# Softmax denominators of an attention layer folded by an accumulating DMA, with smaller edits around it, in a two-layer fp32 kernel

## The chip, the cores and the metric

The kernel runs on one core of one Trainium2 chip, in fp32 throughout. The time is the device time of one execution of the whole program, in microseconds (us); the median of the runs counts. The engines are named as in the profile: PE (TensorE matmul), PEld (its weight loads), DVE (VectorE), ACT (ScalarE), POOL (GpSimd) and SP (SyncE, which issues most of the DMAs). One fp32 matmul instruction appears in the trace as two records, so that counts of records are twice the counts in the code.

## The reference

The input is 16 images of 256 channels and 32 x 32 pixels, that is 16 times a 256 x 1024 matrix. Two layers follow each other:

```python
# layer 0: attention, 4 heads of 64
qkv = (xs @ w_proj + b_proj).reshape(B, S, 4, 192)
q, k, v = split(qkv, 3, axis=-1)
attn = softmax(einsum('bihd,bjhd->bijh', q, k) * SCALE, axis=2)
x = (einsum('bijh,bjhd->bihd', attn, v) @ w_out + b_out + xs)
# layer 1: group norm, attention with 8 heads of 32, group norm, MLP of 1024
x = x + attention(group_norm(x, gn1_w, gn1_b), qkv_w, proj_w, proj_b, phys_bias)
h = gelu(mlp_w1 @ group_norm(x, gn2_w, gn2_b) + mlp_b1)
x = x + (mlp_w2 @ h + mlp_b2)
```

`phys_bias` is one number per head, added to the scores. The MLP is done with seven block products in place of eight (`make_blocks`, `mlp`).

## The kernel before, in words

`first_pass` does all images in one unrolled program. Channels lie on the 128 partitions in two halves (`CC` = 2), pixels in two blocks of 512 (`NT` = 2, `TB` = 512) or eight of 128 (`SB` = 8). Softmax is done without subtracting the maximum; `dsum` and `isum` collect the denominators and their inverses, and at the end one flag tells whether they stayed in range; `general_pass` would run only if they had not.

The order of the instructions is written out by hand. Each attention is a Python generator that yields once per step; `run` (L1036) draws from it, calls `later.tick()` at each step and puts pieces of other work (`fill`) behind the step. `Later.after(n, f)` (L37) runs `f` n ticks later. Each engine takes its instructions in the order so made; the queue of SP is one of them. A few instructions are placed by the tile framework's scheduler where they are likely to be ready, and `tc.issue_after` holds them behind a given instruction.

For each image b the stages are:

* `attention_a` (L384), layer 0, 32 steps: scores (L398), exp on ACT (L406), the sum of the exps over the key blocks on DVE (`es_a`, L431), the weighted values (L419). `cols[0]` = 32 makes other products use 32-column tiles meanwhile.
* The first MLP half of image b-1 (`hidden`: L906, gelu at L919), then query, key and first value products of layer 1 (`qkv_1`, L830).
* `attention_b` (L508), layer 1. An item (t, c) is a block of 512 queries and a half of the channels, that is four heads of 32. The items come in the order (1,0), (0,0), (0,1), (1,1). Each has four steps of two key blocks: scores of four heads on 32 x 64 tiles (L532), exps into `e` tiles (L547), sums over key blocks on DVE into two `es` tiles of 128 x 2 x 512 (`add`, L563), weighted values into `acc` (L584), added up in `res_b` (L595, L597). Behind each step `fill` puts the remaining products of layer 1's query, key and value (`own`), the second MLP half of image b-1 (`m`, L344, with 32-column tiles) and layer 0's query, key and value of image b+1. Only the first and the last image have little of this: the first has `own` alone, the last `own` and three MLP pieces.

After its last key block an item calls `normalise` (L601) one tick later: four matmuls of `eones` (128 x 32, the exponential of the bias) with the four 128 x 512 sums give the denominators `den_b`, each head's on 32 equal rows (L606). `denominators` (L357) then copies `den` to SBUF (L358, ACT), takes one row of each head to a 128 x 16 tile by DMA (L363, SP), one tick later inverts it (L367, DVE), writes it to DRAM (L368, SP), adds to `dsum` and `isum` (L369, L370, POOL) and broadcasts it back over 32 rows each (L373, four DMAs of 64 KB on SP). `scale` (L629) multiplies `res_b` with it and, after the second half of a block, sets off the projection `j` (`out_proj`, L660). The last item's steps fall into the next image's `attention_a`: its projection is handed over and done at step `SB + 4` there (L486).

Loads: `load_x` of the next image (1 MB) and `load_blocks(1, b-1)` (1.79 MB, L278) are written at the start of the loop over b (L1099 to L1103), before `attention_0` of that image; `load_blocks(2, b-1)` is written after the MLP's first half (L1119).

ACT has the functions Exp and Gelu in different tables. The compiler puts an `ACT_TABLE_LOAD` ahead of the first activation of each kind, so one ahead of the gelus and one ahead of the first exp of `attention_b` (listed under L547).

```python
den = bank(f"den_{key}_{i}", 1)
for g in range(G):
    nc.tensor.matmul(den[g * D : (g + 1) * D, :], k["eones"][:, c * G + g],
                     sums[i][g // 2][:, g % 2, :], start=True, stop=True)
```

Of the kernel before, what the change touches and what calls it, by code (L numbers as in the profile page):

```python
# [54 lines left out]
def kernel(  # L55
# [145 lines left out]
    ebias = const.tile([P, HEADS1], F32, name="ebias")  # L201
    eones = const.tile([P, HEADS1, D1], F32, name="eones")

    def exp_bias():
        nc.scalar.activation(ebias, pb, AF.Exp)
        nc.vector.tensor_copy(eones, ebias.unsqueeze(2).to_broadcast([P, HEADS1, D1]))


# [10 lines left out]
    with ExitStack() as first:  # L219
        first_pass(  # L220
            first, tc, x, out,
            dict(
                wp=wp, bqk=bqk, pb=pb, bo=bo, g1w=g1w, g1b=g1b, g2w=g2w,
                g2b=g2b, pjb=pjb, m1b=m1b, m2b=m2b, wo=wo, wq=wq, wpj=wpj,
                m2b2=m2b2, gavg=gavg, mhalf=mhalf, ones=ones, eones=eones,
                bvo=bvo, at_start=at_start, load_rest=load_rest, exp_bias=exp_bias,
                scale_v=scale_v,
                make_blocks=make_blocks,
                in_range=in_range,
            ),  # L230
        )
# [15 lines left out]
def first_pass(ctx, tc, x, out, k):  # L247
# [108 lines left out]

    def denominators(key, den, d, full, waits, then):  # L357
        nc.scalar.copy(d, den)  # L358
# [3 lines left out]
        row = dram.tile([4 * TB // n, n], F32, tag="row", name=f"row_{key}", bufs=4)  # L362
        nc.sync.dma_start(spread, d[::32].rearrange("p (a b) -> p a b", b=w))  # L363

        def invert():
            inverse = work.tile([P, w], F32, tag="inverse", name=f"inv_{key}", bufs=2)
            tc.keep_in_program_order(nc.vector.reciprocal(inverse, spread))  # L367
            nc.sync.dma_start(row.rearrange("r (a b) -> (r a) b", b=w), inverse)  # L368
            nc.gpsimd.tensor_add(dsum, dsum, spread)  # L369
            nc.gpsimd.tensor_add(isum, isum, inverse)  # L370
            num = P * n // (4 * TB)
            for r in range(P // num):
                nc.sync.dma_start(  # L373
                    full[r * num : (r + 1) * num], row[r].partition_broadcast(num)
                )
            later.after(waits[1], lambda: then(full))
# [7 lines left out]
    def attention_a(b, qT, kT, v, project):  # L384
# [3 lines left out]
        res = act.tile([P, CC, S], F32, tag="res", name=f"res_{key}")  # L388
        accs, held, sums = {}, {}, {}

# [18 lines left out]
        def weigh(i, kb, e):  # L409
# [19 lines left out]
            if kb == 1:  # L429
                sums[i] = work.tile([P, 2, TB], F32, tag="es", name=f"es_{key}_{i}", bufs=4)  # L430
            nc.vector.tensor_add(sums[i], held[i] if kb == 1 else sums[i], e)  # L431
# [76 lines left out]
    def attention_b(b, qT, kT, v, project):  # L508
# [3 lines left out]

        items = [(NT - 1, 0)]
        items += [(t, 0) for t in range(NT - 1)] + [(t, 1) for t in range(NT)]
        units = [(i, kb) for i in range(len(items)) for kb in range(0, SB, 2)]
        res, sums = {}, {}

# [35 lines left out]
        def add(i, kb, es, which):  # L553
            if kb == 0 and 0 in which:
                sums[i] = [
                    work.tile([P, 2, TB], F32, tag="es", name=f"es_{key}_{i}_{n}", bufs=4)
                    for n in range(G // 2)
                ]
            for n in which:
                if kb == 0 and n < G // 2:  # L560
                    continue
                d = sums[i][n % 2]
                ins = nc.vector.tensor_add(d, es[n % 2] if kb == 0 else d, es[n])  # L563
# [5 lines left out]
        def result(t):  # L569
            if t < NT - 1 and b == 0:  # L570
                return [
                    work.tile([P, TB], F32, tag="g", name=f"res_{key}_{t}_{c}", bufs=16)
                    for c in range(CC)
                ]
            tag = "res1" if t == NT - 1 else "res" if b < B - 1 else "q0"
            r = act.tile([P, CC, S if tag == "q0" else TB], F32, tag=tag, name=f"res_{key}_{t}")
            return [r[:, c, :TB] for c in range(CC)]

        def weigh(i, kb, es):
# [18 lines left out]
            if kb == SB - 2:  # L598
                later.after(1, lambda: normalise(i, r, i == len(items) - 1))

        def normalise(i, r, last):  # L601
# [3 lines left out]
            for g in range(G):  # L605
                nc.tensor.matmul(  # L606
                    den[g * D : (g + 1) * D, :],
                    k["eones"][:, c * G + g],
                    sums[i][g // 2][:, g % 2, :],
                    start=True,  # L610
                    stop=True,
                )
            full = work.tile([P, TB], F32, tag="full", name=f"rd_{key}_{i}", bufs=1)
            if at_end:
# [83 lines left out]
    def group_norm(key, src, stats, gw, gb, tag, out_tile, wait, then=None):  # L698
# [30 lines left out]
        def variances():  # L729
# [6 lines left out]
            nc.vector.tensor_mul(dv, dv, dv)  # L736
            tv = small.tile([P, CC], F32, tag="tv", name=f"tv_{key}")
            nc.vector.tensor_add(tv, dv, st["mv"][:, :, 1])
            st.update(mean=mean, tv=tv)
            later.after(1 if cols[0] == P else 5, apply)  # L740

        def apply():
# [3 lines left out]
            nc.gpsimd.tensor_tensor(rstd, rstd, k["mhalf"], ALU.pow)  # L746
            a = small.tile([P, CC], F32, tag="ga", name=f"ga_{key}")
            nc.vector.tensor_mul(a, rstd, gw)
            ma = small.tile([P, CC], F32, tag="gma", name=f"gma_{key}")
            nc.vector.tensor_mul(ma, st["mean"], a)  # L750
            c = small.tile([P, CC], F32, tag="gc", name=f"gc_{key}")
            nc.vector.tensor_sub(c, gb, ma)
# [16 lines left out]
    def qkv(key, D, src, weights, b_qk, qT, kT, v_dst):  # L769
# [17 lines left out]

        def v(n):
            ps = single(f"v_{key}_{n}")
            for i in range(2):  # L790
                sb = 2 * n + i
                for cc in range(CC):
# [6 lines left out]
                    )  # L799
            nc.scalar.copy(  # L800
                v_dst()[:, 2 * n : 2 * n + 2],
# [93 lines left out]
    def mlp(b, xb):  # L895
# [45 lines left out]

        def finish(i):
            ps = open_sums.pop(i)
            products_of(i, [(7, ps[:, 0, :], False), (6, ps[:, 1, :], False)])
# [5 lines left out]
            combine((1, 0), (0, 0), False, i)  # L950
            combine((0, 1), (1, 1), False, i)

        hidden = [
# [101 lines left out]

    nothing = work.tile([P, TB], F32, tag="full", name="nothing", bufs=1)
    nc.vector.memset(nothing, 0.0)
# [36 lines left out]
    later.after(2, fold_bias)  # L1094
    later.after(8, k["scale_v"])
    hidden, outputs = [], []
    last = NT * CC * SB // 2 - 1
    for b in range(B):
        if b + 1 < B:  # L1099
            xs[b + 1] = load_x(b + 1)  # L1100
        xn = []
        if b:
            load_blocks(1, b - 1)  # L1103
        run(
# [36 lines left out]
        if not first:  # L1141

            fill = {m: [piece] for m, piece in enumerate(own[:5:2] + own[1::2] + own[6:])}
            fill.update({len(own) + 3 * m: [piece] for m, piece in enumerate(now)})
            now = []
# [28 lines left out]
    for j, (what, most) in enumerate(((dsum, DEN_MAX), (isum, 1.0 / DEN_MIN))):  # L1174
        top = small.tile([P, 1], F32, tag="top", name=f"top_{j}")
        nc.vector.tensor_reduce(top, what, AX.X, ALU.add)
# [4 lines left out]
    nc.vector.tensor_scalar(ok[:32], count, P - 0.5, None, ALU.is_ge)  # L1181
    both = small.tile([P, 1], F32, name="both", bufs=1)
    nc.vector.tensor_mul(both[:32], ok[:32, 0:1], ok[:32, 1:2])
# [294 lines left out]
```

## Time and profile before

| | |
|---|---|
| median of 3 runs | 3666.58 us (3666.36 to 3667.38) |
| the profiled execution, its own time | 3666.7 us |
| its span in the trace | 3664.9 us |
| DVE, ACT, POOL busy | 2658.1, 2154.3, 129.5 us |
| granted PE clock | 0.999 |
| one image in the middle of the run (from one stage to the same stage of the next image) | 226.4 us |
| `den_b` matmuls (L606) | 512 records, 592 ns each |
| ACT_TABLE_LOAD of L547 | 15, of 1283 ns |

Busy is the time in which an engine has at least one instruction of its own running. Four matmuls on different column tiles run beside each other, so the mean time of one record is not what it costs; that is read from the distance between the starts of neighbouring groups. The chain of work goes back from the last instruction, at each step to what released it or to the instruction before it on its engine; a row of it is the start, the length in us, engine, tile, line. In the timeline a row also gives the shapes, the number of records, and in brackets the idle time of the engine before it and what ended that.

### The profile page before, as it was taken

How to read it: one execution, taken by the hardware profiler on the slowest of the kernel's cores; microseconds unless marked ns; L12 is line 12 of the kernel's file. 1: busy time of each engine (PE TensorE's matmuls, PEld its weight loads, DVE VectorE, ACT ScalarE, POOL GpSimd, SP SyncE). 2: the span in 40 equal slices, each digit the busy share in tenths (PEclk: the TensorE clock that was granted, in tenths of full speed). 3: DMA queues.
4: the chain of work that ended last, by engine and by line, in shares of the span. 5: the costliest groups of instructions: out<-in, count | busy, mean ns of one | idle time of the engine just before them, and what ended most of it. 6: DMA issues, size and time to landing. Idle time of an engine off the chain costs nothing.

```text
span 3664.9 us, 79373 instructions
## 1 busy us (share of the span) xinstructions
PE 3632.6 (99%) x34221; PEld 1346.2 (37%) x34221; DVE 2658.1 (73%) x3424; ACT 2154.3 (59%) x2832; POOL 129.5 (4%) x266
## 2 busy tenths in 40 slices
PE   9999999999999999999999999999999999999999
PEld 3433343333433334333343333434334343343433
DVE  4586777767777677776767777677777777767777
ACT  4665657556565655656556565564655656556572
POOL 3000000000000000000000000000000000000000
PEclk9999999999999999999999999999999999999999
DMA  4000110101101011010110101101011010100100
GB/s 147 10 17 29 55 33 14 51 30 54 33 14 51 30 54 33 14 51 31 53 33 20 51 27 51 33 19 50 27 51 33 19 50 29 50 33 31 47 28 27
DMA packets 66549, 138.36 MB, mean 38 GB/s; under 512 B 35630, under 2 KB 36398, under 8 KB 61966
## 3 DMA queue, kind: packets, MB, share of 16 engines
q1 hardware_dynamic: 63116, 126.64, 10.7%
q8 instruction: 270, 4.42, 0.5%
q0 software_dynamic: 1328, 6.17, 0.5%
q14 instruction: 89, 0.73, 0.1%
q10 hardware_dynamic: 1746, 0.40, 0.1%
HBM read 111.17 MB, written 21.23 MB: 36 GB/s over the span
## 4 chain that ended last, share of the span: by engine, by line
PE 91%; DVE 4%; ACT 3%; DMA 1%; issue 1%; SPq 0%; ACTq 0%; POOL 0%; DVEq 0%
PE s_a L398 12%; PE acc_b L584 12%; PE s_b L532 12%; PE acc_a L419 12%; PE m L344 10%; PE m L906 9%; PE qk_a L344 6%; PE qk_b L344 5%; PE v_a L344 3%; PE j L344 3%; PE v_b L344 2%; ACT e_b L547 2%; PE o L344 2%; PE den_b L606 1%; DVE g L962 1%
## 5 line engine op out<-in xcount | busy, mean ns | idle before, releaser
L563 DVE TENSOR_TENSOR es_b<-es_b,e_b 128x1024 f32<-128x1024 f32 x768 | 899.3, 1219 | 243.8 <-ACT e_b L547 243.8
L547 ACT ACTIVATE e_b<-s_b 128x1024 f32<-128x1024 f32 (+1 forms) x1280 | 982.9, 864 | 132.2 <-PE s_b L532 132.0
L406 ACT ACTIVATE e_a<-s_a 128x1024 f32<-128x1024 f32 x512 | 521.2, 1025 | 360.0 <-PE s_a L398 347.6
L398 PE MATMUL s_a<-q,k 64*64 64x512 f32 x4096 | 544.3, 593 | 0.0
L419 PE MATMUL acc_a<-e_a,v 64*64 64x512 f32 x4096 | 540.1, 589 | 0.0
L532 PE MATMUL s_b<-q,k 32*64 32x512 f32 x8192 | 519.7, 600 | 4.9 <-DVE res_b L597 1.6
L431 DVE TENSOR_TENSOR es_a<-es_a,e_a 128x1024 f32<-128x1024 f32 x384 | 473.9, 1234 | 64.8 <-ACT e_a L406 41.2
L584 PE MATMUL acc_b<-e_b,v 128*32 128x512 f32 x4096 | 492.1, 598 | 0.0
L344 PE MATMUL m<-g,w 128*32 128x512 f32 (+1 forms) x3320 | 404.3, 592 | 0.0
L532 PEld LDWEIGHTS s_b<-q,k 32*64 32x64 f32 x8192 | 170.9, 130 | 321.3 <-issue 130.9
L419 PEld LDWEIGHTS acc_a<-e_a,v 64*64 64x64 f32 x4096 | 187.9, 133 | 251.5 <-issue 218.4
L398 PEld LDWEIGHTS s_a<-q,k 64*64 64x64 f32 x4096 | 175.9, 133 | 246.7 <-issue 193.1
L563 DVE TENSOR_TENSOR es_b<-e_b,e_b 128x1024 f32<-128x1024 f32 x128 | 150.8, 1220 | 153.4 <-ACT e_b L547 153.4
L906 PE MATMUL m<-gn_h,w 128*128 128x512 f32 x512 | 243.7, 604 | 5.7 <-DVE g L932 3.3
L584 PEld LDWEIGHTS acc_b<-e_b,v 128*32 128x32 f32 x4096 | 108.5, 109 | 357.5 <-ACT e_b L547 194.7
L344 PE MATMUL qk_a<-x,wp 128*32 128x512 f32 (+1 forms) x1856 | 235.1, 593 | 4.1 <-ACT k L784 4.1
L344 PE MATMUL qk_b<-gn_g,wq 128*32 128x512 f32 (+1 forms) x1280 | 234.0, 592 | 0.0
L597 DVE TENSOR_TENSOR res_b<-res_b,acc_b 128x512 f32<-128x512 f32 x192 | 131.8, 686 | 129.8 <-PE acc_b L584 129.8
L344 PEld LDWEIGHTS m<-g,w 128*32 128x32 f32 (+1 forms) x3320 | 121.4, 112 | 262.3 <-issue 235.3
L962 DVE TENSOR_TENSOR g<-g,g 128x512 f32<-128x512 f32 x320 | 206.3, 681 | 4.0 <-ACT g L919 2.8
L906 PE MATMUL m<-hs,w 128*128 128x512 f32 x384 | 177.9, 592 | 0.1
L919 ACT ACTIVATE g<-g,m1b 128x512 f32<-128x512 f32 x128 | 92.2, 722 | 99.3 <-DVE g L946 72.2
(147 smaller groups left out, 2803.6 us busy)
## 6 DMA issues: line engine op xcount, KB each, us to landing
w<-w_kept SPq DMA_DIRECT2D x30, 1792.0 KB
d_a<-row_a SPq DMA_DIRECT2D x64, 256.0 KB
rd_b<-row_b SPq DMA_DIRECT2D x252, 64.0 KB
out_dram<-x SPq DMA_DIRECT2D x63, 256.0 KB
x<-in_x_dram SPq DMA_DIRECT2D x30, 512.0 KB
w_kept<-w_made POOLq DMA_DIRECT2D x2, 1792.0 KB, 6.0
w_made<-in_L_conv_mlp_w_dram POOLq DMA_DIRECT2D x8, 256.0 KB, 6.1
x<-in_x_dram SPq DMA_DIRECT2D x4, 256.0 KB
```

The costliest lines, as they stand in the source:

```text
L344: nc.tensor.matmul(o[sl], w[:, sl], r, **flags)
L398: nc.tensor.matmul(s[h : h + HALF, g, :], kT[g * D : (g + 1) * D, c, kb * P + h : kb * P + h + HALF], qT[g * D : (g + 1) * D, c, t * TB : ...
L406: nc.scalar.activation(e, s, AF.Exp, scale=float(D) ** -0.5)
L419: nc.tensor.matmul(accs[i][h][g * D : (g + 1) * D, :], v[h * HALF : (h + 1) * HALF, kb, c * 2 + g], e[h * HALF : (h + 1) * HALF, g, :], st ...
L431: nc.vector.tensor_add(sums[i], held[i] if kb == 1 else sums[i], e)
L532: nc.tensor.matmul(outs[g][h : h + HALF, :], kT[g * D : (g + 1) * D, c, k0 : k0 + HALF], qT[g * D : (g + 1) * D, c, t * TB : (t + 1) * TB] ...
L547: nc.scalar.activation(to, s, AF.Exp, scale=float(D) ** -0.5)
L563: ins = nc.vector.tensor_add(d, es[n % 2] if kb == 0 else d, es[n])
L584: nc.tensor.matmul(acc[g * D : (g + 1) * D, :], v[:, kb + m, c * G + g], es[2 * m + g // 2][:, g % 2, :], start=(m == 0), stop=(m == 1),)
L597: nc.vector.tensor_add(r, r, acc)
L906: nc.tensor.matmul(ps, blocks[1][number - 1][:, i * P : (i + 1) * P], inputs[b][number], start=first, stop=True, skip_group_check=not first,)
L962: (nc.vector.tensor_add if plus else nc.vector.tensor_sub)(d, d, gs[(*what, i)])
```

## The change

Three of an image's four items get their denominators in another way. `fold` copies the sums of the lower 64 partitions of `es` (64 x 4 x 512) over 128 partitions (128 x 2 x 512) with a DMA on SP, and a second DMA, issued by POOL, adds the upper 64 partitions to it. Three ticks after `fold`, `normalise_folded` multiplies the result with `folded`, whose columns say which head a partition holds: eight matmuls of 128 columns in place of four of 512. A head's denominators lie on 8 equal rows now, and the 512 queries as four groups of 128 rows by 128 columns; so `denominators` takes 16 rows to the 128 x 16 tile and writes the inverses with four DMAs (`parts`). The wait between the broadcast and `scale` is 2 ticks (4 for the third item). The last item of each image, and the third of the last image, are done as before. `packed` lies in the buffer with the tag "res", which the group norm's output `gn_g` holds before; that output is read by the products `qk_b` and `v_b`.

With it: the items go in the order (0,0), (0,1), (1,0), (1,1), and the results take other buffers; `full` has two buffers; the large loads are written 14 ticks into `attention_a`, behind the last broadcast; the copy of the first `v_b` goes to DVE; behind the last gelu of `hidden` a one-column Exp (`back_to_exp`) is put on ACT; in the first and last image `own` is spread in another way over the steps, and its last piece (`qk_b`) then stands at step 5. Some small tiles are shared.

```diff
+    def fold_ones():
+        nc.gpsimd.memset(folded, 0.0)
+        g_num = P // D1
+        w = D1 // g_num
+        for c in range(HEADS1 // g_num):
+            for g in range(g_num):
+                nc.gpsimd.dma_start(
+                    folded[g // 2 :: 2, c, g % 2, g * w : (g + 1) * w],
+                    eones[g // 2 :: 2, c * g_num + g, :w],
+                )
...
-    def denominators(key, den, d, full, waits, then):
+    def denominators(key, den, d, full, waits, then, parts=1):
...
-        nc.sync.dma_start(spread, d[::32].rearrange("p (a b) -> p a b", b=w))
+        nc.sync.dma_start(
+            spread, d[:: 32 // parts].rearrange("p (a b) -> p a b", b=w)
+        )
...
+            if parts > 1:
+                num = P // parts
+                for r in range(parts):
+                    nc.sync.dma_start(
+                        row[:, r * n // parts : (r + 1) * n // parts].rearrange(
+                            "g (a b) -> g a b", b=w
+                        ),
+                        inverse[r * num : (r + 1) * num],
+                    )
...
-                nc.sync.dma_start(
+                spread_out["last"] = nc.sync.dma_start(
...
-        items = [(NT - 1, 0)]
-        items += [(t, 0) for t in range(NT - 1)] + [(t, 1) for t in range(NT)]
+        items = [(t, c) for t in range(NT) for c in range(CC)]
...
             if kb == SB - 2:
-                later.after(1, lambda: normalise(i, r, i == len(items) - 1))
+                last = i == len(items) - 1
+                if last or b == B - 1 and t == NT - 1:
+                    later.after(1, lambda: normalise(i, r, last))
+                else:
+                    fold(i, r)
+
+        def fold(i, r):
+            if i == 0:
+                packs.append(act.tile([P, 4, TB], F32, tag="res", name=f"packed_{key}"))
+            packed = packs[0][:, i % 2 * 2 : i % 2 * 2 + 2]
+            nc.sync.dma_start(packed, sums[i][:HALF])
+            nc.gpsimd.dma_start(packed, sums[i][HALF:], accum_op=ALU.add)
+            later.after(3, lambda: normalise_folded(i, r, packed))
+
+        def normalise_folded(i, r, packed):
+            c = items[i][1]
+            q = TB // G
+            den = bank(f"den_{key}_{i}", 1)[:, :q]
+            for m in range(2):
+                for n in range(G):
+                    nc.tensor.matmul(
+                        den[n * D : (n + 1) * D, :], k["folded"][:, c, m],
+                        packed[:, m, n * q : (n + 1) * q], start=m == 0, stop=m == 1,
+                    )
+            full = work.tile([P, TB], F32, tag="full", name=f"rd_{key}_{i}", bufs=2)
+            denominators(
+                f"{key}_{i}", den, full[:, :q], full, (1, 2 if i < 2 else 4),
+                lambda full: scale(i, r, False, full), G,
+            )
...
+            copy = nc.vector.tensor_copy if not n and b_qk is None else nc.scalar.copy
...
+            if i == n4 - 1:
+                later.after(2, back_to_exp)
...
+        def back_to_exp():
+            one = small.tile([P, 1], F32, tag="part", name=f"one_{b}")
+            nc.scalar.activation(one, gs[1, 1, n4 - 1][:, :1], AF.Exp, scale=0.0)
...
+    later.after(9, k["fold_ones"])
...
-        if b + 1 < B:
-            xs[b + 1] = load_x(b + 1)
+        def load_next(b=b):
+            if not b:
+                xs[1] = load_x(1)
+                return
+            with tc.issue_after(spread_out["last"].ins):
+                load_blocks(1, b - 1)
+                if b + 1 < B:
+                    xs[b + 1] = load_x(b + 1)
+
+        later.after(14, load_next)
...
-            fill = {m: [piece] for m, piece in enumerate(own[:5:2] + own[1::2] + own[6:])}
+            fill = {0: own[:1], 1: own[1:3], 2: own[4:5], 3: own[5:6], 4: own[3:4], 5: own[6:]}
```

## The prediction

> **What bounds the kernel now.** I read the page first: busy times, then the chain that ended last.
>
> ```profile
> PE 3632.6 (99%) x34221; PEld 1346.2 (37%) x34221; DVE 2658.1 (73%) x3424; ACT 2154.3 (59%) x2832; POOL 129.5 (4%) x266
> ...
> PEclk9999999999999999999999999999999999999999
> ...
> PE 91%; DVE 4%; ACT 3%; DMA 1%; issue 1%; SPq 0%; ACTq 0%; POOL 0%; DVEq 0%
> ```
>
> PE has work nearly always, at full clock, and holds 91% of the chain. So a gain is either a matmul that is no longer done, or one of the few moments in which PE waits. The chain of one image from the middle, in order of time, shows what the denominators cost there:
>
> ```profile
> 1255.40 1.90 PE s_b L532 x32
> 1257.30 1.85 PE acc_b L584 x16
> 1259.15 0.86 PE den_b L606 x8
> 1260.01 3.43 PE m L344 x32
> 1263.45 1.90 PE s_b L532 x32
> ```
>
> Each step runs matmul to matmul without a gap, 7.19 us a step where nothing is added (1281.58 to 1288.77, from one `m` to the next `den_b`); an item adds 0.86 us. Third, the timeline where attention_b begins, the one place in an image where PE stands still:
>
> ```profile
> 1227.36 1.97 PE L532 MATMUL s_b<-q,k 32*64 32x512 f32 x32
> ...
> 1228.07 1.28 ACT L547 ACT_TABLE_LOAD   x1
> 1229.37 3.84 ACT L547 ACTIVATE e_b<-s_b 128x512 f32<-128x512 f32 x5
> 1230.02 1.93 PE L344 MATMUL v_b<-wq,gn_g 128*32 128x256 f32 x32 [0.68 <-ACT e_b L547]
> ...
> 1233.05 0.63 ACT L800 COPY v<-v_b 128x512 f32<-128x512 f32 x1
> ...
> 1233.73 1.98 PE L532 MATMUL s_b<-q,k 32*64 32x512 f32 x32
> ```
>
> The first exps wait for the table, `v_b` waits for an exp to free its bank (0.68 us), and the next scores wait for the copy of `v_b` behind the exps. The waits on PE's own row agree: `v_b` behind `e_b` is the longest, 10.2 us in 15 times.
>
> **The change part by part.** All against the profiled execution, 3666.7 us (1.8 us around its span; the median of the runs shown is 3666.58, the same).
>
> *Folded matmuls.* Removed per item: 4 matmuls of 512 columns, four column tiles beside each other, two records each: 0.86 us. Added: 8 of 128 columns, so each tile passes 4 records of 128 columns for 2 of 512, half the columns. That columns set the price shows in the chain: 32 records of 256 columns (`v_b`) take 1.73 us, 32 of 512 (`m`) take 3.43. So 0.43 us. Bounds: 0.43, and 0.86 from `den_a` (L450), which has as many instructions as the folded form and costs 0.86. I take 0.43, since `den_a` has 256 columns and fits the column rate itself. There are 3 folded items in 15 images and 2 in the last. In the 14 middle images all is on PE's path: 42 x 0.43 = 18.1 us. In the first and last image ACT paces most steps (PE waits for exps at 170.96 below), and I count nothing. ACT's copy of `den` shrinks from 619 ns; it isn't on the path.
>
> The Trainium skill, "TensorE: Matmul & The Clock Gate", section "Back-to-back issue gap", speaks against short matmuls: streams of load and matmul are said to come every 81 ns at 128 columns, where the isolated gap is 56. As an estimate from it, 4 records deep at that surplus of 25 ns make 0.1 us more, and 4 us less gain in all. The row of 256 columns shows no such surplus; no run here has 128.
>
> *The Exp put behind the last gelu.* The load (1.28 us) moves from 1228.07 to behind the last gelu, which ends at 1222.21. ACT is idle 1.13 us ahead of each of the next copies, so it fits beside PE's `qk_b` (7 us). Then the first exp starts when its scores are there: a step later exps start 1.13 us after `s_b` (1233.73, 1234.86), which makes 1228.49 for 1229.37. That is 0.88 us, and `v_b` and the next `s_b` follow the exps. 15 images: 13.2 us. Bounds: 0 if ACT's copies then hold PE, 1.28 if all of the load counts. The copy given to DVE falls into a DVE idle time of 9.38 us. In the last image the same Exp also stands in the tail on ACT; beside 24 us of unbroken PE products it costs nothing.
>
> The skill, "ScalarE: Activation LUTs", section "What ACT_TABLE_LOAD costs", puts a switch at 2.66 us, load and drain. The rows show 1.28 and an exp 0.02 us later. By the page this term would be up to 15 x 2.66, an estimate of 40 us; the measured row decides.
>
> *The two DMAs of a fold.* 512 KB by SP, then 512 KB added by POOL. In the middle images they lie under two steps. For the second item (old order) the last sum ends at 1285.75, `den_b` stood at 1288.77, and the folded one comes two ticks later, at 1303.2: 17.4 us of cover. The trace has no accumulating DMA. Nearest rows: 512 KB of `d_a<-row_a` 4.3 us; POOL's 256 KB loads 6.1 us, its 1 KB loads from 4.3; `sp_b` on SP 2.0 (1260.84 to 1262.83). Low end 2.0 + 4.3 = 6.3 us, high end 4.3 + 2 x 6.1 = 16.5 if reading two sources doubles POOL's time. I take 4.3 + 6.1 = 10.4, the rows nearest in size. All lie inside 17.4, so the middle images pay nothing.
>
> *The first and last image pay.* `packed` takes the buffer of `gn_g`, whose last reader is the `qk_b` now at step 5, and the folded `den_b` of item 0 is due at step 6: one `s_b` and one `acc_b` later. Rows of the first image:
>
> ```profile
> 165.37 1.90 PE L344 MATMUL qk_b<-gn_g,wq 128*32 128x512 f32 x16
> 167.20 1.97 PE L532 MATMUL s_b<-q,k 32*64 32x512 f32 x32
> 169.11 1.92 PE L584 MATMUL acc_b<-e_b,v 128*32 128x512 f32 x16
> 170.96 3.12 PE L532 MATMUL s_b<-q,k 32*64 32x512 f32 x32
> 174.01 1.92 PE L584 MATMUL acc_b<-e_b,v 128*32 128x512 f32 x16
> ```
>
> From the end of `qk_b` (167.1) to the `acc_b` of the step after: 6.9 us. With the pair of DMAs lasting D, `den_b` starts at D, 0.43 + about 1.9 for the scores, so that `acc_b` comes at D + 2.4: a loss of D - 4.5. Behind the waiting matmul stands all of PE's queue, and ACT, which paces these steps, runs dry. D = 10.4: 5.9 us in each of two images, 11.8. Bounds: 1.8 and 12 each. The three later folds of these two images have about 10.7 us (a sum ends at 175.46, `den_b` stood at 175.75, two steps of some 5 us more follow): 0 at 10.4, D - 10.7 each beyond, 5.8 at the high end.
>
> *At nothing.* SP: three more issues per fold for the inverses, 0.34 us each, in 7.19 us steps; `row` and the broadcasts land within the two ticks of 14 us. POOL: the accumulating DMA waits ahead of `dsum` and `isum`, for which nobody waits but the flag at the end; the group norm's power on POOL comes an attention later. Loads behind the last broadcast: 2.8 MB then have some 40 us until `hidden`, and go at 400 KB per us in the DMA times; what they no longer delay is DVE's `res_b` (waits for `rd_b`, 47.9 us in 14 times) in attention_a, where DVE has 1.23 us of sums per 1.72 us step, so PE gains nothing. If that cover were gone, PE would wait up to 4.7 us an image. `fold_ones` runs on POOL in the first image, far ahead of its use. The new spread of `own`: some 1 us either way.
>
> **Sum:** 18.1 + 13.2 - 11.8 = 19.5. 3666.7 - 19.5 = 3647.2, so 3647 us.
>
> **The rivals.**
>
> *The pair is quick* (D near 6.3 to 8): loss 1.8 to 3.5 in the two images, 31.3 - 3.6 = 27.7 at best: 3639 to 3643. For it: 8 KB trips of 2.0 us and loads at 400 KB per us. Against: POOL's 4.3 us at the least.
>
> *The pair is long* (12 to 14.5): 15 to 20 us lost on item 0 of the two images, 4 to 11 on their later folds: 31.3 - 19 = 12.3 to about 0, so 3654 to 3667.
>
> *The short matmuls save nothing* (0.86 stays, bound by instructions): 13.2 - 11.8 = 1.4, so 3665; no change. For it: `den_a`'s 16 records. Against: the 256-column rows.
>
> *Slower: PE waits for the accumulating DMA in every image.* In-order PE stands at `den_b` 42 times if D exceeds 17.4. The end images alone turn the sign at 14.5 (3677 at 16.5); beyond 17.4 each us costs 42 more. D = 20: 31.3 - 31 (item 0 twice) - 27.9 (three later folds) - 2.6 x 42 = -137, so 3804. For it: no row with addition, and a second source to read. Against: only doubling POOL's row reaches 16.5.
>
> *It doesn't do what it says*: the folded products stand in the code order two steps behind the item, so this is out but for the cases above.
>
> **How the numbers follow.** About 0.2% (7 us) is what a measurement can tell from no change. Forecast (D of 8 to 12, 3643 to 3654) 0.42; quick 0.29; long 0.11, half of it faster (0.05), the rest same (0.06); no saving 0.07, same; slower 0.11. Faster: 0.42 + 0.29 + 0.05 = 0.76. Same: 0.06 + 0.07 = 0.13. Slower: 0.11. The range leaves out the last two cases (0.18): 3637 to 3664; 2 us at the low end are for the spread of `own`.
>
> **What would show it.** Right: `den_b` of 0.43 us in the chain; the table load right behind the last gelu, and no wait of `v_b` for `e_b`; the image's period down from 226.4 to 224.3 us; two waits of PE of some 6 us on the accumulated tile, in the first and last image alone. Wrong: `den_b` groups of 0.6 us or more; waits of PE for that DMA in the middle images; no wait in the end images (the pair is quick); DVE late in attention_b, so that `j` waits.

## The result and the profile after

The changed kernel takes 3675.78 us (median of 13 runs, 3674.66 to 3679.81), the kernel before 3666.58 (13 runs, 3664.54 to 3667.77): a ratio of 1.0027, 95% interval 1.0019 to 1.0036. It is 9 us slower where 19.5 us less were forecast. The profiled execution took 3677.3 us, its span is 3675.3.

The first page hardly shows it. PE is as busy as before, and every slice of the clock row is a 9:

```profile
PE 3627.0 (99%) x34597; PEld 1357.1 (37%) x34597; DVE 2668.4 (73%) x3440; ACT 2131.0 (58%) x2833; POOL 217.4 (6%) x322
...
PEclk9999999999999999999999999999999999999999
...
PE 92%; DVE 5%; DMA 2%; ACT 0%; issue 0%; SPq 0%; ACTq 0%; POOL 0%; DVEq 0%
```

So I laid the two traces side by side by stage, from the first `s_b` or `s_a` of one to that of the next:

| stretch (us) | before | after | difference |
|---|---|---|---|
| the 14 middle images, in all | | | -29.0 |
| `attention_b` of the first image and the `attention_a` after it | 192.0 | 215.3 | +23.2 |
| last image, first `s_b` to last product | 168.3 | 180.2 | +11.8 |
| last product to the end of the span | 4.9 | 8.9 | +4.0 |
| start | | | +0.3 |

Before rounding they sum to 10.4, the difference of the spans. The middle images do what was forecast, 2.1 us an image; 1.4 of the 29.0 us is another matter, a wait of DVE for `d_a<-row_a` that stands in the third image of the kernel before and not here (more on it at e3). The chain of work there, in order of time:

```profile
1285.23 1.85 PE acc_b L604 x16
1287.09 0.44 PE den_b L639 x16
1287.53 3.43 PE m L357 x32
```

`den_b` is 0.44 for 0.86 us and nothing around it waits. All of PE's waits for `packed_b` (three, 16.0 us) fall in the end images. The whole loss lies at the two ends of the run. PE in the first image, at the first folded item:

```profile
163.68 1.98 PE L560 MATMUL s_b<-q,k 32*64 32x512 f32 x32
165.58 1.92 PE L604 MATMUL acc_b<-e_b,v 128*32 128x512 f32 x16
175.17 1.08 PE L639 MATMUL den_b<-packed_b,folded 128*32 128x128 f32 x16 [7.66 <-DMA packed_b<-es_b]
176.18 3.79 PE L560 MATMUL s_b<-q,k 32*64 32x512 f32 x32
```

This is the wait that was forecast, 7.66 us here and 7.43 in the last image:

```profile
3532.90 1.08 PE L639 MATMUL den_b<-packed_b,folded 128*32 128x128 f32 x16 [7.43 <-DMA packed_b<-es_b]
3533.91 4.14 PE L560 MATMUL s_b<-q,k 32*64 32x512 f32 x32
```

The row behind it says more: the same 32 records of `s_b` that took 1.98 us ahead of the wait take 3.79 here, 4.14 there. Asked for the stretches around it in steps of 3.41 us, the trace gives the reason (columns: stretch; its length, then busy time and records of PE, PEld, DVE, ACT, POOL; granted clock; DMA share; GB/s):

```profile
169.24:172.66 3.42, 0.00 (x0) 0.00 (x0) 2.43 (x3) 0.00 (x0) 0.52 (x1) 1.00 0.78 111
172.66:176.07 3.41, 0.90 (x16) 0.66 (x16) 0.00 (x0) 0.00 (x0) 0.00 (x0) 0.50 0.38 42
176.07:179.48 3.41, 3.41 (x36) 1.59 (x32) 0.15 (x1) 1.53 (x4) 0.21 (x1) 0.50 0.05 7
179.48:182.90 3.42, 3.42 (x34) 0.86 (x34) 2.09 (x3) 2.57 (x3) 0.00 (x0) 1.00 0.00 0
196.55:199.96 3.41, 1.66 (x22) 0.59 (x18) 1.76 (x3) 1.42 (x3) 0.00 (x0) 1.00 0.16 50
199.96:203.38 3.42, 2.70 (x30) 0.91 (x30) 3.42 (x5) 0.68 (x2) 0.22 (x1) 0.50 0.02 5
```

The granted clock is 0.50 for 6.8 us behind the wait, and again from 200.0 us on, behind a stretch in which PE was busy 1.66 of 3.41 us. There are four such stretches within the run: 6.8, 6.8 and 3.4 us in the first image, 10.2 in the last; 27.3 us in all at half clock. Before, there was none between start and tail. A slice of the page is 92 us long and rounds them away.

What made PE idle near 200 us is a second wait, on another engine. All engines of the first image:

```profile
186.01 0.56 SPq L629 DMA_DIRECT2D packed_b<-es_b  x1
...
186.62 3.92 SPq L388 DMA_DIRECT2D row_b<-inv_b  x4
...
191.79 4.17 SPq L400 DMA_DIRECT2D rd_b<-row_b  x4
...
198.20 0.69 DVE L679 TENSOR_TENSOR res_b<-res_b,rd_b 128x512 f32<-128x512 f32 x1 [4.07 <-DMA rd_b<-row_b]
...
200.68 3.71 PE L560 MATMUL s_b<-q,k 32*64 32x512 f32 x30 [1.52 <-DVE res_b L617]
```

The second item's 512 KB copy stands on SP's queue ahead of the first item's four small writes. These then take 3.92 us to issue, the broadcasts 4.17. For the third item, with no copy close ahead, it is 2.49 and 1.70:

```profile
240.84 2.49 SPq L388 DMA_DIRECT2D row_b<-inv_b  x4
...
244.50 1.70 SPq L400 DMA_DIRECT2D rd_b<-row_b  x4
```

The multiplication by the inverses, `scale`, stands on DVE two ticks behind the inversion, and in this image a tick is some 5 us: DVE has inverted at 185.90, stands at the multiplication 8.2 us later and waits 4.07 us, for the second item 5.36. Behind it in DVE's order is the `res_b` that frees `acc_b`'s bank, so PE waits too.

Third, the tail. All engines at the end:

```profile
3645.44 1.28 ACT L1005 ACT_TABLE_LOAD   x1
3646.74 0.20 ACT L1005 ACTIVATE one<-g 128x1 f32<-128x1 f32 x1
...
3649.36 0.16 DVE L1237 TENSOR_REDUCE top<-dsum 128x1 f32<-128x16 f32 x1
...
3666.34 0.22 PE L1241 MATMUL count<-ok,ones 128*32 128x2 f32 x2
```

The Exp of the last image writes a tile of the tag "part", and so does `top` now, the first step of the range flag. `top` comes behind the Exp, `count` behind the last product, and the program ends on the flag. Before, `count` was hidden among the products:

```profile
3609.38 0.22 PE L1180 MATMUL count<-ok,ones 128*32 128x2 f32 x2
```

### The profile page after: what moved, and what is told of

The parts are those of the page before. It is cut to its first block, busy times and chain, and to the rows that moved or that the text cites. A ratio compares the mean times of both kernels' runs of the same rounds, so it can differ in the third digit from the quotient of the medians.

```text
span 3675.3 us, 80535 instructions
## 1 busy us (share of the span) xinstructions
PE 3627.0 (99%) x34597; PEld 1357.1 (37%) x34597; DVE 2668.4 (73%) x3440; ACT 2131.0 (58%) x2833; POOL 217.4 (6%) x322
## 4 chain that ended last, share of the span: by engine, by line
PE 92%; DVE 5%; DMA 2%; ACT 0%; issue 0%; SPq 0%; ACTq 0%; POOL 0%; DVEq 0%
PE s_b L560 13%; PE acc_b L604 12%; PE s_a L425 12%; PE acc_a L446 12%; PE m L357 10%; PE m L954 7%; PE qk_b L357 6%; PE qk_a L357 6%; PE v_a L357 3%; PE v_b L357 3%; PE j L357 3%; PE o L357 2%; DVE g L1016 1%; PE den_a L479 1%; DMA d_a<-row_a 1%; DVE x L719 1%
## 5 line engine op out<-in xcount | busy, mean ns | idle before, releaser
L560 PE MATMUL s_b<-q,k 32*64 32x512 f32 x8192 | 528.8, 605 | 9.5 <-DVE x L719 2.9
```

What stands on the lines that cost most here:

```text
L560: nc.tensor.matmul(outs[g][h : h + HALF, :], kT[g * D : (g + 1) * D, c, k0 : k0 + HALF], qT[g * D : (g + 1) * D, c, t * TB : (t + 1) * TB] ...
```

## The experiments

My theory after reading the traces: all of the loss comes from the folds of the two end images (the wait, the half clock behind it, DVE's wait) and from the Exp in the tail. The rivals: the new order of the items and the new spread of `own` cost there; or the DMAs cost everywhere. Times are medians, beside 3675.8 (changed) and 3667 to 3668 (before, in the same sessions); the ratio is to the kernel before, with its 95% interval.

**Nothing folded in the end images** (e1).

```diff
-                if last or b == B - 1 and t == NT - 1:
+                if last or b in (0, B - 1):
                     later.after(1, lambda: normalise(i, r, last))
```

> The changed kernel, but in the first and the last image no item is folded: all four go the old way through es_b and eones. Theory (the whole loss lies in the folds of these two images: PE's wait for packed, the half clock behind it, DVE's wait for the broadcasts behind the second 512 KB DMA): attention_b of the first image back from 108.1 to about 90.5 us, attention_a of the second image from 107.1 to 101.8, the last image from 180.2 to about 168.5, the clock at 1.0 but for the start and the end; 3675.8 - 17.6 - 5.3 - 11.7 = 3641 us (3637 to 3646). Rival (the loss in the two images comes from the new order of the items and the new spread of own, not from the folds): these stretches keep their lengths and the time stays at 3670 to 3677. Rival (the extra DMAs cost everywhere): 3660 to 3668, with the middle images longer than the 224.34 us read from the changed kernel's own trace.

Measured: 3655.58 us, 0.9967 (0.9955 to 0.9979). That is 20 us better, but 15 short of the theory: the first stretch is still 8.0 us longer than before, the last image 3.7, the tail 3.5. The theory fell as a full account; the folds of the end images are the larger part. What remains, PE in the first image:

```profile
193.94 3.62 PE L357 MATMUL j<-res_b,wpj 128*32 128x512 f32 x32
197.49 1.95 PE L560 MATMUL s_b<-q,k 32*64 32x512 f32 x24
200.86 1.31 PE L560 MATMUL s_b<-q,k 32*64 32x512 f32 x8 [1.43 <-DVE x L719]
202.10 3.34 PE L604 MATMUL acc_b<-e_b,v 128*32 128x512 f32 x16
```

With the new order both halves of the first block are done after two items, so its projection `j` stands in the middle of the stage; it holds a bank until DVE, full of sums, gets to `x`. `acc_b` is at half clock behind it (3.34 for 1.92). Before, `j` stood at the last step, where PE, as I read it, would have waited for DVE anyway.

**Order and spread in the end images as before** (e5; e1 with it), and with no Exp in the tail (e6).

```diff
+        if b in (0, B - 1):
+            items = [(NT - 1, 0)]
+            items += [(t, 0) for t in range(NT - 1)] + [(t, 1) for t in range(NT)]
...
-            fill = {0: own[:1], 1: own[1:3], 2: own[4:5], 3: own[5:6], 4: own[3:4], 5: own[6:]}
+            fill = {m: [piece] for m, piece in enumerate(own[:5:2] + own[1::2] + own[6:])}
```

> As the kernel with the unfolded end images (3655.6 us), and there the items also go in the order of before, (1,0), (0,0), (0,1), (1,1), with the products of own spread as before. With the folds gone, the first image with the following attention_a was still 8.0 us longer than before (199.99 for 192.03) and the last image 3.7 (172.08 for 168.33). Theory (the order and the spread cost this: the projection j of the first block stands in the middle of the stage, where DVE is behind, in place of its end, and own's pieces double up at step 1): 3655.6 - 8.0 - 3.7 = 3643.9 us (3641 to 3647). Rival (it comes from the shared buffers es and full, or the loads, which this run keeps as changed): 3655.6, no change.

> The run just above and, with it, no Exp behind the last gelu of the last image. If the losses add up: 3643.9 - 4.0 = 3639.9 us (3637 to 3643), which leaves the gain of the 14 middle images alone, 29 us read from the two traces, beside 2 us of first-image differences. Rival (the flag at the end is hidden once the last image is shorter): 3644.

Measured: 3644.96 us, 0.9940 (0.9927 to 0.9954), and 3642.75, 0.9934 (0.9921 to 0.9948). e6 gains 2.2 of the 4.0 us: in its trace 7.2 us still lie behind the last product, and why is open (e12 below, with the same rows at its end, has 4.9). The first image is back to its length of before, the last 0.9 us shorter. Order and spread cost 10.6 us with nothing folded in the end images.

**Which of the two** (e13: e1 with `j` put off by four ticks to the last step; e14: e1 with the old order and the new spread).

```diff
-                    later.after(1, issue)
+                    later.after(5 if b in (0, B - 1) and t < NT - 1 else 1, issue)
```

> The changed kernel with the end images unfolded (3655.6 us), the new order of items and the new spread of own kept, and there the projection j of the first block put off by four ticks, to the last step, where it stood before the change. Theory (in the unfolded end images it is j's place that costs: 5.5 us of the 8.0 in the first image, and most of the 4.6 that the last image lost beside the run with order and spread as before, 3645.0): 3655.6 - 8 = 3647.5 us (3645 to 3650). Rival (the spread of own costs, its doubled step 1 and the later query products): 3652 to 3656.

> The end images unfolded and their items in the order of before, with the new spread of own. Beside 3645.0 us (order and spread as before) and 3655.6 (both new). Theory (the order costs, through j's place; the spread costs 2.5 us in the first image and about 1 in the last): 3648 us (3646 to 3650.5). Rival (the spread is the cause): 3653 to 3656. Rival (the spread costs nothing by itself): 3645.

Measured: 3650.42, 0.9953 (0.9939 to 0.9966), and 3648.16, 0.9947 (0.9933 to 0.9960). So the spread costs 3.2 of the 10.6 us (1.7 in each image by the traces) and the order 7.4, of which 5.2 go with `j` alone; 8 were expected of it.

**No Exp behind the last gelu of the last image** (e2).

```diff
-            if i == n4 - 1:
+            if i == n4 - 1 and b < B - 1:
                 later.after(2, back_to_exp)
```

> The changed kernel, but the Exp behind the last gelu isn't done in the last image, where no exp follows. Theory (that one-column tile shares the tag part with the two sums of the range flag, so they wait for it at 3646.9 us, the count stands behind the last product at 3666.3 and the program ends on the flag, 8.9 us after PE's last product; before it was 4.9): the count is back in the middle of the products, the program ends 4.9 us after PE's last product: 3675.8 - 4.0 = 3671.8 us (3671 to 3673). Rival (the flag is late for another reason, such as the last image's folded denominators, or what follows the flag runs beside the last store): 3675.8, no change.

Measured: 3671.75, 1.0014 (1.0005 to 1.0023); `count` is at 3611.7, 4.9 us lie behind the last product. As expected.

**The first image's `packed` in the free buffer of `x`** (e4), **then `scale` a tick later** (e7), **or `j` alone a tick later** (e9); the diffs in this order.

```diff
-                packs.append(act.tile([P, 4, TB], F32, tag="res", name=f"packed_{key}"))
+                packs.append(
+                    act.tile([P, 4, TB], F32, tag="res", name=f"packed_{key}") if b
+                    else act.tile([P, 4, TB], F32, tag="x", name=f"packed_{key}", bufs=3)
+                )
```

```diff
-                f"{key}_{i}", den, full[:, :q], full, (1, 2 if i < 2 else 4),
+                f"{key}_{i}", den, full[:, :q], full, (1, (2 if b else 3) if i < 2 else 4),
```

```diff
-                    later.after(1, issue)
+                    later.after(1 if b else 2, issue)
```

> The changed kernel with the first image's packed in the third buffer of x, which is free then, in place of the buffer that gn_g holds until the last qk_b. Theory (the pair of DMAs takes some 11.5 us and only its late start, behind gn_g's last reader at 163.6, makes PE wait): SP issues the first copy at about 157 us, den_b of the first item waits 0 to 1.5 us in place of 7.66, the half-clock stretch behind it goes; 3675.8 - 6.5 - 2.2 = 3667 us (3664 to 3670); the second half-clock stretch at 200 us stays, since it comes from DVE's wait for the broadcast. Rival (the accumulating DMA is itself slow in the first image, beside the load of the weights and x): den_b still waits 5 us or more, 3673 to 3677.

> The changed kernel with the first image's packed in the free buffer of x (3667.5 us), and in the first image the multiplication by the broadcast inverses of the first two items stands three ticks behind the inversion in place of two. Theory (steps of 5 us there, where middle images have 7.2; DVE stands at this multiplication for 4.1 and 5.4 us, because the inverses' four small writes are issued behind the next item's 512 KB copy on SP's queue and take 3.9 us for 1.4; the sums behind it are late, PE waits and the clock halves for some 10 us): these DVE waits shrink to under 1 us, the half-clock stretches in the first image go, 3667.5 - 5 = 3662.5 us (3660 to 3665). Rival (the first image is bound by DVE's own work, 93% busy, so that one wait only takes another's place): 3666 to 3668.

> The changed kernel with the first image's packed in the free buffer of x (3667.5 us), and in the first image the projection j of the first block one tick later; the multiplication by the inverses stays where it was. In the run with that multiplication a tick later (3653.6 us) j moved by the same tick, from ahead of the last step's scores to behind them. Theory (j's place is the larger part: its bank is freed by DVE only behind the item's sums, so the last scores wait for DVE and the clock halves; in the last gap PE waits for DVE anyway): 8 to 10 us of the 13.9 come with j alone, 3658 us (3656 to 3661). Rival (DVE's waits of 4.1 and 5.4 us for the broadcasts are the cause, j only follows them): 0 to 3 us, 3664 to 3668.

Measured: 3667.49 (1.0000, 0.9991 to 1.0009), 3653.57 (0.9966, 0.9952 to 0.9979) and 3665.38 (0.9993, 0.9984 to 1.0002). The first agrees: the first image's wait and the half clock behind it cost 8 to 9 us. The second gave 13.9 us where I expected 5, and with 1.3 us over before the first image is whole. In e7 `j` moved by the same tick. The third run tells why it isn't mainly `j`: by the traces `j` alone gives 3.2 us of the 12.8 by which this stretch shrank, where I had expected 8 to 10. The other 9.6 need the later multiplication. That tick takes both waits from DVE and, with them, three 3.4 us windows at half clock. The rest of the first image after e7, on PE:

```profile
209.03 2.40 PE L560 MATMUL s_b<-q,k 32*64 32x512 f32 x32
211.36 1.92 PE L604 MATMUL acc_b<-e_b,v 128*32 128x512 f32 x16
213.10 3.62 PE L357 MATMUL j<-res_b,wpj 128*32 128x512 f32 x32
216.53 1.90 PE L604 MATMUL acc_b<-e_b,v 128*32 128x512 f32 x16
```

`j` stands ahead of the last `acc_b`, as before the change, and none of these rows waits.

**All folds kept, each loss mended** (e11: e7 and e2, and in the last image `den_b` of the first item two ticks later, `scale` one).

```diff
-            later.after(3, lambda: normalise_folded(i, r, packed))
+            later.after(5 if i == 0 and b == B - 1 else 3, lambda: normalise_folded(i, r, packed))
```

> All folds of the change are kept and the losses are mended one by one: in the first image packed in the free buffer of x and the multiplication (and j) a tick later, as in the run of 3653.6 us; in the last image the folded den_b of its first item two ticks later, and the multiplication a tick later there too; no Exp behind the last gelu of the last image. Theory (the last image loses its 7.4 us wait and the half clock behind it, 5 us, and the tail 2 to 4): 3653.6 - 11 - 2.2 = 3640.5 us (3638 to 3645), which equals the kernel whose end images aren't folded (3642.75) within 3 us, as the folds there gain nothing. Rival (the last image has less slack than the first, and the later den_b only moves the wait to the multiplication by the inverses): 3646 to 3651.

Measured: 3643.95, 0.9937 (0.9924 to 0.9951). That is e6's time within the noise: with later dates the folds cost little in the end images. The last image stays 5.4 us longer than before; 3.7 of it stood in e1 too, with nothing folded there.

**PE kept busy in the wait** (e3: five matmuls in both end images; e15: eight, in the last image of e7).

```diff
+            if i == 0 and b in (0, B - 1):
+                busy = bank(f"busy_{key}", 1)
+                for _ in range(5):
+                    nc.tensor.matmul(
+                        busy, k["wq"][:, 0, :P], k["wq"][:, 0, :TB], start=True, stop=True
+                    )
             den = bank(f"den_{key}_{i}", 1)[:, :q]
```

> The changed kernel with five more matmuls of 128 x 128 by 512 whose result nobody reads, ahead of the folded den_b of the first item in the first and the last image, so that PE works while it waits for packed. Theory (the wait itself is the DMAs' time and stays, but the half clock from 172.7 to 179.5 and from 3528.0 to 3538.2 us comes from PE standing still): den_b starts at the same times, some 11.5 us after the SP copy is issued; the clock stays 1.0 there and the s_b behind it takes 1.97 us in place of 3.79 and 4.14; of the 4.3 and 5.3 us of work done at half clock, half is saved: 2.2 + 2.6 = 4.8, so 3671.0 us (3669 to 3673.5). Rival (the slow s_b comes from the DMAs or from ACT, not from PE's standing still): 3675.8 or more, the same half-clock stretches. Against both: matmuls that are too long for the wait would push den_b back, 0.86 us each.

> The kernel whose first image is mended (3653.6 us; packed in x's buffer, the multiplication a tick later), with eight more matmuls of 128 x 128 by 512, 6.9 us that nobody reads, in the last image's wait of 7.42 us for packed. The wait ends as before, with the DMAs. Theory (the half clock from 3506.8 to 3513.6 us comes from PE standing still): no half clock there, den_b 0.65 in place of 1.08 and the s_b behind it 1.97 in place of 3.44, the last image's stretch 179.4 - 1.9 = 177.5 us, the time 3651.7 (3650 to 3653). Rival (the clock falls there for another reason, or the slow s_b is the DMAs' doing): the same half-clock stretch and 179.4 us or more.

Measured: 3680.38 (1.0034, 1.0022 to 1.0046) and 3654.84 (0.9966, 0.9954 to 0.9978). On the time both miss; the traces tell more. In e3 the first image has no half clock behind the wait any more and its stretch is 1.6 us shorter; in the last image the filler left 3.56 us of wait, and half clock followed. The total rose through other things: the start 1.0, and 1.6 to 1.9 us in `attention_a` of the fifth, ninth and thirteenth image, where DVE waits for `d_a<-row_a` (in the fifth the broadcast was issued 3.3 us after the row's write, 1.4 in the changed kernel). The same delay, 0.8 to 1.6 us, shows in two images of e1, e5, e6, e13 and e14, in three of e12, in one of e4, and in the third image of e8, of e10 and of the kernel before; not in e7, e9 or e11. So the change didn't bring it; its cause is open. In e15 the wait is filled, and the stretches read:

```profile
3503.80:3507.20 3.40, 3.40 (x15) 1.42 (x8) 2.97 (x4) 1.75 (x2) 0.95 (x1) 1.00 0.29 55
3507.20:3510.60 3.40, 3.40 (x9) 1.49 (x9) 1.38 (x2) 0.00 (x0) 0.00 (x0) 1.00 1.02 135
3510.60:3514.00 3.40, 3.40 (x39) 1.13 (x44) 0.00 (x0) 0.27 (x1) 0.00 (x0) 1.00 0.05 8
```

The DMAs are as busy as in an unfilled wait (DMA share 1.02), PE is busy, and the clock stays at 1.00. Behind the filler `den_b` takes 0.65 and `s_b` 2.41 us; in e7, with the same wait unfilled, it was 1.08 and 3.44. So the half clock is that of PE's standing still, not of the DMAs. The gain is small: the last image 0.9 us shorter for 1.9 expected, lost in a start that was 2.5 us later.

**Nothing folded anywhere** (e8), and **the Exp alone in the kernel before** (e10); the second diff is to the kernel before.

```diff
-                if last or b == B - 1 and t == NT - 1:
+                if True:
```

```diff
+            if i == n4 - 1 and b < B - 1:
+                later.after(2, back_to_exp)
...
+        def back_to_exp():
+            one = small.tile([P, 1], F32, tag="one", name=f"one_{b}")
+            nc.scalar.activation(one, gs[1, 1, n4 - 1][:, :1], AF.Exp, scale=0.0)
```

> The changed kernel with no item folded in any image: all denominators by eones over the whole es_b, the rest as changed. Beside the kernel with the unfolded end images (3655.6 us) it shows what the folds are worth in the 14 middle images. Theory (den_b 0.44 in place of 0.86 us, 42 items, all else hidden): 3655.6 + 17.6 = 3673.2 us (3671 to 3676). Rival (the extra DMAs and the longer chains slow the middle images and eat part of it): 3657 to 3668. Rival (folds give more than the matmuls, since PE's bank and DVE are relieved): above 3678.

> The kernel before with one edit of the change: the one-column Exp behind the last gelu, in all images but the last. Theory (the table load goes behind the last gelu, where ACT waits for PE anyway, and the first exps of attention_b start 0.88 us sooner): 15 x 0.88 = 13.2, so 3667.2 - 13.2 = 3654 us (3652 to 3657). The run with nothing folded showed 0.88 us an image less in the middle images, but with all other edits in. Rival (a part of that comes from the copy of the first v_b on DVE, which is not in this run: it took 0.63 us on ACT behind the exps): 3656 to 3663. Rival (ACT's copies behind the load hold PE): no change. The Trainium skill, 'ScalarE: Activation LUTs', section 'What ACT_TABLE_LOAD costs', would make it up to 15 x 2.66 = 40 us, an estimate from its figure: 3627.

Measured: 3666.14 (0.9999, 0.9990 to 1.0008) and 3654.14 (0.9963, 0.9950 to 0.9977). By its time e8 is where the first rival had it. Against e1 the traces show 1.21 us more in `attention_b` of nearly every middle image, 15.5 in all. The time shows only 10.6, since e1 pays elsewhere (1.7 in the first image, 3.3 in the delays just named, 1.7 at the end) and e8 pays 1.3 in one such delay; whether the folds' DMAs have a part in e1's delays is open. e10 gains what was forecast, 0.88 to 0.90 us in nearly every image, by ACT's rows:

```profile
1220.97 1.28 ACT L957 ACT_TABLE_LOAD   x1
...
1227.23 3.83 ACT L547 ACTIVATE e_b<-s_b 128x512 f32<-128x512 f32 x5 [0.43 <-PE s_b L532]
```

**The large loads at the start of the image again, in e6** (e12).

```diff
...
-        later.after(14, load_next)
+        if b + 1 < B:
+            xs[b + 1] = load_x(b + 1)
         xn = []
+        if b:
+            load_blocks(1, b - 1)
```

> The kernel with the end images as before and no Exp in the tail (3642.75 us), with the large loads (x of the next image, the MLP's blocks) issued at the start of the image again, as before the change. Theory (the move is worth nothing: what waits for rd_b behind them is DVE, which has slack there): 3642.75, within 1.5 us. Rival (the early loads delay the last item's broadcasts, DVE comes late to the sums of attention_a and PE waits): 1 to 4.7 us in each of 14 images, 3657 to 3709.

Measured: 3641.17, 0.9930 (0.9916 to 0.9943), not to be told from e6. It is the best version here, 0.7% under the kernel before.

## Why the prediction was wrong, step by step

* **Folded matmuls, 18.1 us.** Right: `den_b` 0.44, so no surplus for short matmuls; 1.21 us an image for its three items, 15.5 in all (e8 against e1).
* **The Exp behind the last gelu, 13.2.** Right in 15 images (e10: 3668.2 to 3654.1). The Trainium skill, "ScalarE: Activation LUTs", section "What ACT_TABLE_LOAD costs", would have made it up to 40 us, an estimate from its 2.66. The gain alone can't set the load's price, since the exps can't start ahead of their scores. ACT's rows of the kernel before can: the copy ahead of the load ended 0.01 us before it, the load took 1.28, and the exp began 0.02 later.
* **"In the last image the same Exp ... costs nothing."** Wrong: it costs 4.0 us (e2). I counted ACT's and PE's work beside it, not the tile: a shared tag put the flag behind it.
* **The pair, D = 10.4, hidden in the middle images.** Right: 11.4 and 11.1 us from SP's issue to `den_b` in the end images, no wait in the middle.
* **The first and last image pay 11.8.** The mechanism was right and the place too; its price was not. The step that failed is "`den_b` starts at D, 0.43 + about 1.9 for the scores": these rows are for full clock, and behind 7 us of standing still they took 1.08 and 3.79. Without the wait (e4) the first image's stretch was 9.2 us shorter, where the sum had 5.9; in the last image the folds cost 8.1 in all (e1).
* **Later folds there, "0 at 10.4, D - 10.7 each beyond".** With the measured D that is 0.7. Nearly right for PE at `den_b` (0.94 us at the second item), wrong in all: see the next point.
* **"At nothing": "`row` and the broadcasts land within the two ticks of 14 us".** This failed worst, 12.8 us in the first image (e7 against e4; 3.2 of it come with `j` alone). Two ticks are 14 us in a middle image; in the first DVE stood there after 8.2, and I had moved the writes behind a 512 KB copy on the same queue without counting it: the four took 3.9 us to issue, not 0.34 each. By the chain DVE hardly counts, but its order holds PE's banks.
* **"The new spread of `own`: some 1 us either way."** 3.2 us (e14 against e5). The new order of the items, which I gave no term, costs 7.4 more in the end images with nothing folded, most of it through `j`.
* **Loads and SP's issues in the middle images.** Right for the loads, nothing (e12). SP's issues took longer than I had them, but PE waits for none of these DMAs in the middle images.

Of the rivals, "PE waits in every image" was out, as argued. The sign turned as in "the end images alone", but not by its price: D stayed under 14.5.

## What to carry to other kernels

A delay counted in steps is a delay in time only where the step has the length you took: look up every tick in the image with the shortest steps, and what stands ahead on the same queue. When PE is made to wait, add what the next records cost at half clock. And a tile tag that is shared is an order between its users, also at the very end, where nothing hides it.

## What the runs showed of the hardware

* The clock is granted in stretches of 3.41 us or a multiple (3.4, 6.8, 10.2 here). The Trainium skill, "TensorE: Matmul & The Clock Gate", section "What's actually happening", has this free-running window of 3413 ns; the rows agree.
* That page's section "Why this matters for your kernels" advises no gaps of PE over some 3 us. Here less was enough: ahead of the stretch at 200.0 us the gaps were 0.94 and 1.52 us, but PE was busy in only 1.66 of the window's 3.41. Over the traces of the two kernels and e1 to e12, start and tail left out, 17 of 19 full-clock windows with PE busy for 53% or less, and 3 with 58 to 63%, were followed by half clock; many others of 56% and more were not.
* Four 2 KB writes take SP 3.9 us to issue right behind a 512 KB copy, and the four 64 KB broadcasts that follow, beside POOL's addition, 4.2 us; without a copy close ahead 2.5 and 1.7 us. Which of the two DMAs slows the broadcasts isn't told apart here.
* A DMA that adds 512 KB into SBUF took 6.6 us from POOL's issue to landing (median of 47), close to the 6.1 of POOL's 256 KB loads.
